# Mask transfers of one or two steps, and the queue of one block's inverse denominators, in a two-layer graph attention kernel

## The chip, the cores and the metric

The kernel runs on one core of a Trainium2 chip. The metric is the time in microseconds of one execution on the device, and the median over the runs is compared. A core has five engines with queues of their own: TensorE (PE in the profile, its weight loads PEld), VectorE (DVE), ScalarE (ACT), GpSimd (POOL) and SyncE (SP, which computes nothing and issues transfers). PE, DVE and ACT compute here; POOL mostly issues transfers, some of which add into their destination.

## The reference

There are 4096 nodes with 512 features in 4 heads of 128, and one adjacency matrix for both layers. Layer 0 is an encoder and a decoder with the same attention weights, layer 1 an ordinary graph attention:

```python
h = jnp.maximum(_layernorm(x), 0.0)
Xw = einsum('hnd,hde->hne', Xh, W)                   # Xh: h by heads
sig = sigmoid(f1[:, :, None] + f2[:, None, :])       # f1, f2: scores of a node, by head
att = masked_softmax(sig, adj != 0)                  # both patterns are adj
Xa = einsum('hij,hjd->hid', att, Xw)                 # encoder attention
emb = _mlp_block(_batchnorm(Xa), enc_mlp_W, ...)     # elu, residual, batch norm
Y = einsum('hij,hjd->hid', att, emb by heads)        # decoder attention, the same att
out = _mlp_block(elu(Y @ W^T), dec_mlp_W, ...)
x = x + out
# layer 1
h = jnp.maximum(_layernorm(x), 0.0)
feats = einsum('nf,hfo->hno', h, W1)
logits = leaky_relu(e_s[:, :, None] + e_n[:, None, :], 0.2) - 1e10 * (1 - A)
x = x + relu(softmax(logits) @ feats + b)
```

## The kernel before

All three attentions are one function, `attention`, called as "enc", "dec" and "gat". It works in eight **blocks**, one for each head `h` and half `tb` of the target nodes (`TB` = 2048), and a block in 32 **steps** `j` of 128 source nodes. A step makes one tile `e` of 128 x 2048 weights: in the encoder and the decoder ACT computes a tanh (line 579) and an exponential (580), and DVE multiplies by the mask (581); in the last attention ACT does one operation (1073) and DVE one with the mask in it (1074). Then PE multiplies `e` with the step's values (474 and 477 in the encoder and the last attention, 336 in the decoder).

**The masks.** Before the encoder begins, POOL's queue copies the adjacency from 32-bit floats to bytes in DRAM (`copy_adjacency`, eight casting transfers). SP loads the masks back: `mask_tile` takes one of three buffers, each of which holds the masks of two steps, and `load_mask` (line 217) fills it with one transfer of 512 KB. In every fifth step (`KEEP` = 5) the encoder stores its weights in DRAM, and the decoder reads these back instead of computing them; such a step needs no mask in the decoder, but its pair's transfer brings both. Three tiles for the encoder's first steps are loaded early, as `masks0`.

**The denominators.** The column sums of `e` are made in three ways, which lists of steps choose: POOL issues transfers that add halves of `e` into a sum (line 497, the "moved" steps), DVE adds `e` (505 and 507), or PE multiplies by ones (272). A block's sums are ready when it ends, and `ending` spreads the rest over the steps of the next block with `at(j, ...)`: `denominators` copies the sums from PSUM and stores them (`dens`), `columns` loads them as a column (`dcol`), `invert_them` inverts them on DVE (288 and 289), `inverses` stores the inverses (`rinvs`, line 292), and four `spread` load them, repeated for all partitions, into `rb` tiles (297). Then `scaled` (698) and `statistics` (701) work on the block's outputs on DVE. In the encoder and the decoder these small transfers are issued by POOL (`hop`), in the last attention by ACT. For the encoder's first block, whose ending runs in its second block, `slack` = 4 sets the steps back, and `dens` and `dcol` go on SP's queue; `rinvs` and `rb` go on POOL's.

The order within each engine's queue is laid out by the framework's scheduler from the order of the code, the dependencies, its own estimates of time and the explicit `issue_after` edges; an engine takes its queue in that order. `a_load` is the latest mask load, and the next row's load and a few extras are placed after it.

Of the kernel before, what the change touches and what calls it, by code (L numbers as in the profile page):

```python
# [45 lines left out]
TB = 2048  # L46
# [3 lines left out]
MG = 8  # L50
# [26 lines left out]
INVERT = 4  # L77
# [13 lines left out]
def kernel(ctx, tc, x, xT, adjT, w0, w0T, v0, wencT, wdecT, vecs, w1, w1T, a1, outT):  # L91
    nc = tc.nc
# [76 lines left out]
    masks = [[dram.tile([P, MG * TB], U8, name=f"mask{t}_{g}") for g in range(NJ // MG)] for t in range(NTB)]  # L169
# [41 lines left out]
    def mask_tile(keep):  # L211
        return keep.tile([P, 2 * TB], U8, name="a", bufs=3)

    def load_mask(a, tb, j):

        k = j % MG // 2
        return nc.sync.dma_start(a, masks[tb][j // MG][:, k * 2 * TB:(k + 1) * 2 * TB])

    @contextmanager
    def pinned(behind):  # L220
# [7 lines left out]
    def attention(what, keep, pools, weights, values, row_of, out, finish, ebufs, modes=None, invert=None,  # L228
                  kept=None, sums=None, sums2=None, extras={}, row0=None, masks0=(), in_parts0=1,
# [24 lines left out]
        spool, made, masks0 = pools, 0, list(masks0)  # L254
# [12 lines left out]
        hop = nc.scalar if kept is None else nc.gpsimd  # L267
# [20 lines left out]
            nc.vector.tensor_scalar(dcols[0], dcols[0], invert[0], None, invert[1])  # L288
            nc.vector.reciprocal(dcols[0], dcols[0])

        def inverses(h, tb, dcols):
            hop.dma_start(rinvs[h][tb].rearrange("o (p k) -> (o p) k", k=TB // P), dcols[0])

        def spread(h, tb, s):

            rb = spool.tile([P, IB], FP, name="rb", bufs=3 if fast is None else 2)
            hop.dma_start(rb, everywhere(rinvs[h][tb], 0, s * IB, IB))  # L297
            return rb

        def at(j, f, *args):  # L300

            later.setdefault(j, []).append(lambda: f(*args))

        def ending(h, tb, po, den, slack):

            outs = [out(spool, h, tb, s, po[s]) for s in range(SB)]
            if den is not None:

                dcols = []
                at(INVERT, denominators, h, tb, den, nc.sync if slack else hop)  # L310
                at(INVERT + (0 if hop is nc.gpsimd else 3) + slack // 2, columns, h, tb, dcols, nc.sync if slack else hop)
                at(INVERT + slack + (6 if hop is nc.gpsimd else 7), invert_them, dcols)
                at(INVERT + slack + (6 if hop is nc.gpsimd else 10), inverses, h, tb, dcols)
            rbs = {}
            for s, o in enumerate(outs):

                j = INVERT + slack + (7 if hop is nc.gpsimd else 11) + s % 2 + s // 2 * (7 if hop is nc.gpsimd else 5)
                at(j, lambda s=s: rbs.update({s: spread(h, tb, s)}))
                for k, f in enumerate(finish):
                    at(j + (6 + k if hop is nc.gpsimd else 3 + 3 * k),  # L320
                       lambda f=f, s=s, o=o: f(spool, h, tb, s, o, rbs[s], False))
# [78 lines left out]
        for n, (h, tb) in enumerate(blocks):  # L400
# [13 lines left out]
            adds, held, stores, at_end, next_row, two_masks = [], [], [], [], None, (None, None)  # L414
            for j in range(NJ):
# [11 lines left out]
                if store and kept == "read":  # L427
                    a_load = nc.sync.dma_start(e, ekeep[h][tb][j // KEEP])
                else:
                    if two_masks[0] != j // 2:  # L430
                        if masks0:
                            two, a_load = masks0.pop(0)
                        else:
                            two = mask_tile(keep)
                            a_load = load_mask(two, tb, j)
                        two_masks = j // 2, two
                    a = two_masks[1][:, j % 2 * TB:(j % 2 + 1) * TB]

                    with pinned([*(products_of[:1] if kept == "read" and n == 0 and j < 8 else ()),
                                 *(behind if n == 0 and j < EP else ())]):  # L440
                        products_of = weights(e, rowb, a, j, h, SB if NJ * n + j < in_parts0 else 1)


                    if stores and (store if n > 1 else j % KEEP == KEEP - 3):
                        k, t = stores.pop()
                        (nc.sync if n > 1 else nc.scalar).dma_start(ekeep[h][tb][k], t)
                    if store:
                        stores.append((j // KEEP, e))
# [137 lines left out]
    with tc.tile_pool(name="keep", bufs=1) as keep:  # L586

        with tc.tile_pool(name="f_small", bufs=1) as small, tc.tile_pool(name="f_work", bufs=2) as work:
# [29 lines left out]
            for ib in range(NIB):  # L618
                st = work.tile([P, C, 6], FP, name="st")
                mv = work.tile([P, C, 2], FP, name="mv")  # L620
                rstd = work.tile([P, C], FP, name="rstd")

                def deviations(lo, hi):

                    with pinned([first_hn] if ib == 1 or lo == 1 else []):
                        for c in range(lo, hi):
                            nc.vector.bn_stats(st[:, c, :], xs[ib][:, c, :])
                    for c in range(lo, hi):
                        nc.vector.bn_aggr(mv[:, c, :], st[:, c, :])
                    return rsqrt(rstd[:, lo:hi], mv[:, lo:hi, 1], LN_EPS)  # L630

                last_dve = deviations(0, 1 if ib == 0 else C)
                hT = work.tile([P, C, IB], FP, name="hT")
                for c in range(C):
                    if ib == 0 and c == 1:
                        last_dve = deviations(1, C)
                    by_pool = c == C - 1
                    hn = work.tile([P, F], FP, name="hn", tag="hnp" if by_pool else "hn")
                    made = (nc.gpsimd if by_pool else nc.vector).tensor_scalar(
                        hn, xs[ib][:, c, :], mv[:, c, 0:1], rstd[:, c:c + 1], ALU.subtract, ALU.mult)  # L640
                    if ib == 0 and not by_pool:
                        first_hn = made

                    if by_pool and ib > 0:
                        with tc.issue_after(made.ins):
                            copy_adjacency(ib - 1, half_loaded)
                            if ib == NIB - 1:
                                copy_adjacency(ib, half_loaded)
                    pt = bank().rearrange("p (f n) -> p f n", n=P)
                    for fb in range(C):  # L650
                        last_pe = nc.tensor.transpose(pt[:, fb, :], hn[:, fb * P:(fb + 1) * P], ident)
                    nc.scalar.activation(hT[:, :, c * P:(c + 1) * P], pt, AF.Relu)
                if ib == 0:

                    pw = bank1()
                    with tc.issue_after(last_pe.ins):
                        for h in range(H):
                            nc.tensor.matmul(pw[:, 2 * h:2 * h + 2], w0Ts[:, h, :], v0s[:, h, :],
                                             start=True, stop=True)
                    pwh = pw[:, 0:2 * H].rearrange("p (h s) -> p h s", s=2)  # L660
                    with tc.issue_after(last_dve.ins):
                        nc.vector.tensor_copy(w0x[:, :, D], pwh[:, :, 0])
                        nc.vector.tensor_scalar_mul(w0x[:, :, D + 1], pwh[:, :, 1], 0.5)
                for c in range(C):
                    j = ib * C + c
                    for k in range(2):
                        pv = heads_of(bank())
                        for h in range(2):
                            nc.tensor.matmul(pv[:, h, :], hT[:, 2 * k + h, c * P:(c + 1) * P], w0x[:, 2 * k + h, :],
                                             start=True, stop=True)  # L670

                        by_dve = ib + k >= NIB - 1
                        copied = (nc.vector.tensor_copy if by_dve else nc.scalar.copy)(
                            RS[:, 2 * k:2 * k + 2, j * D:(j + 1) * D], pv[:, :, 0:D])
                        if not by_dve:
                            last_copy = copied
                        nc.vector.tensor_copy(scores_of(j, k), pv[:, :, D:DX])
                if ib == SB - 1:
                    store_rows(rows[0], targets(0))
                    row0 = keep.tile([P, TB], FP, name="rowb", bufs=2)  # L680
                    row0_load = load_row(row0, rows[0], 0)
                    with tc.issue_after(row0_load.ins):
                        masks0 = []
                        for j in range(0, 6, 2):
                            a = mask_tile(keep)
                            masks0.append((a, load_mask(a, 0, j)))
            store_rows(rows[1], targets(1))


# [467 lines left out]
```

## Time and profile before

| what | value |
|---|---|
| median of 3 runs | 3191.95 us (3190.81 to 3193.84) |
| profiled execution | 3189.99 us, its span 3188.2 us |
| encoder attention, from its first product | 64.7 to 1034.9 us |
| decoder attention | 1174.7 to 2016 us |
| last attention | 2268 us to the end |
| mask loads | 384 of 512 KB, 4.9 us to land (median) |
| accumulating transfers of the encoder's sums | 142 of 512 KB, 7.6 us to land (median) |
| granted TensorE clock | 0.999 |

Lines of a timeline give the start and the duration in microseconds, the engine and line, the operation, its output and inputs, the number of merged instructions, and in square brackets the idle time of that engine just before, with what ended it. "DMA rb<-rinvs" as a releaser means that a transfer from `rinvs` into `rb` landed. The lines of a wait summary give a total in microseconds, the number of times, and the longest.

### The profile page before, as it was taken

How to read it: one execution, taken by the hardware profiler on the slowest of the kernel's cores; microseconds unless marked ns; L12 is line 12 of the kernel's file. 1: busy time of each engine (PE TensorE's matmuls, PEld its weight loads, DVE VectorE, ACT ScalarE, POOL GpSimd, SP SyncE). 2: the span in 40 equal slices, each digit the busy share in tenths (PEclk: the TensorE clock that was granted, in tenths of full speed). 3: DMA queues.
4: the chain of work that ended last, by engine and by line, in shares of the span. 5: the costliest groups of instructions: out<-in, count | busy, mean ns of one | idle time of the engine just before them, and what ended most of it. 6: DMA issues, size and time to landing. Idle time of an engine off the chain costs nothing.

```text
span 3188.2 us, 29265 instructions
## 1 busy us (share of the span) xinstructions
PE 3137.4 (98%) x10555; PEld 1369.9 (43%) x10555; DVE 2933.7 (92%) x2227; ACT 2574.2 (81%) x1830; POOL 520.1 (16%) x678
## 2 busy tenths in 40 slices
PE   7999999999999999999999999999999999999999
PEld 6444444434444463333333333458544444444444
DVE  7999999999999778999999999785699999999998
ACT  7999999999999449999999999466755656665663
POOL 3001211211211000010100100026312222122211
PEclk9999999999999999999999999999999999999999
DMA  9999978988988015545555555331579999899986
GB/s 214 204 199 248 270 200 231 260 224 229 264 225 214 24 47 165 168 156 187 172 176 172 171 183 162 92 112 64 155 187 233 217 222 240 219 212 236 229 209 173
DMA packets 167330, 603.07 MB, mean 189 GB/s; under 512 B 20672, under 2 KB 24016, under 8 KB 151184
## 3 DMA queue, kind: packets, MB, share of 16 engines
q0 software_dynamic: 70912, 231.92, 37.6%
q1 hardware_dynamic: 84112, 345.11, 31.5%
q10 hardware_dynamic: 12160, 24.16, 2.2%
q8 instruction: 83, 1.36, 0.2%
q14 instruction: 63, 0.52, 0.0%
HBM read 392.05 MB, written 84.30 MB: 149 GB/s over the span
## 4 chain that ended last, share of the span: by engine, by line
PE 69%; issue 11%; DVE 9%; DMA 6%; ACT 4%; POOL 0%; DVEq 0%; SPq 0%; ACTq 0%; POOLq 0%
PE ps L477 29%; PE ps L336 22%; PE ps L734 7%; PE den L336 3%; PE ps L979 3%; DVE e L581 3%; DMA w<-e 3%; DVE acc L507 3%; ACT e L579 2%; DMA acc<-e 2%; PE den L272 1%; ACT e L580 1%; DVE e L1074 1%; DVE R L507 1%; PE ps L817 1%
## 5 line engine op out<-in xcount | busy, mean ns | idle before, releaser
L477 PE MATMUL ps<-e,R 128*128 128x512 f32 x3992 | 1734.8, 594 | 24.4 <-DVE e L581 20.1
L477 PEld LDWEIGHTS ps<-e,R 128*128 128x128 f32 x3992 | 753.5, 190 | 1001.8 <-issue 926.0
L581 DVE TENSOR_TENSOR e<-e,a 128x2048 f32<-128x2048 f32 (+1 forms) x470 | 1048.1, 2259 | 70.5 <-ACT e L580 68.1
L579 ACT ACTIVATE e<-rowb,score 128x2048 f32<-128x2048 f32 (+1 forms) x470 | 909.6, 1970 | 21.8 <-PE ps L336 7.6
L580 ACT ACTIVATE e<-e 128x2048 f32<-128x2048 f32 (+1 forms) x470 | 866.8, 1880 | 3.4
L336 PE MATMUL ps<-e,R 128*64 128x512 f32 x2624 | 746.8, 592 | 1.6 <-DVE e L581 1.5
L1073 ACT ACTIVATE e<-rowb,nq,jcol 128x2048 f32<-128x2048 f32 x224 | 458.6, 2088 | 274.6 <-DMA w<-e 154.8
L1074 DVE SCALAR_TENSOR_TENSOR e<-e,jcol,a 128x2048 f32<-128x2048 f32 (+1 forms) x265 | 591.6, 2264 | 2.9 <-ACT e L1073 2.0
L336 PEld LDWEIGHTS ps<-e,R 128*64 128x64 f32 x2624 | 242.1, 137 | 319.6 <-issue 316.0
L507 DVE TENSOR_TENSOR R<-R,e 128x2048 f32<-128x2048 f32 x124 | 282.5, 2278 | 0.0
L507 DVE TENSOR_TENSOR acc<-acc,e 128x2048 f32<-128x2048 f32 x122 | 278.6, 2284 | 1.0
L497 POOL DMA_DIRECT2D w<-e x178 | 147.5, 834 | 613.8 <-DMA w<-e 390.4
L497 POOL DMA_DIRECT2D acc<-e x142 | 118.0, 873 | 701.2 <-DMA acc<-e 213.6
L734 PE MATMUL ps<-R,w 128*128 128x512 f32 x512 | 220.8, 593 | 0.6 <-DVE w L708 0.6
L734 PEld LDWEIGHTS ps<-R,w 128*128 128x128 f32 x512 | 97.1, 190 | 123.0 <-issue 116.9
L336 PE MATMUL den<-e,R 128*64 128x512 f32 x320 | 149.8, 592 | 0.0
L336 PE MATMUL ps<-e,w 128*64 128x512 f32 x288 | 138.1, 592 | 0.7 <-DVE e L581 0.7
L297 POOL DMA_DIRECT2D rb<-rinvs x60 | 34.8, 584 | 521.3 <-DVE R L698 450.2
L979 PE MATMUL ps<-w1x,hT 128*128 128x260 f32 x512 | 115.5, 384 | 0.7 <-ACT hT L957 0.7
L336 PE MATMUL ps<-t,w 128*64 128x512 f32 x336 | 111.3, 593 | 1.1 <-DVE t L345 1.1
L979 PEld LDWEIGHTS ps<-w1x,hT 128*128 128x128 f32 x512 | 96.6, 190 | 18.8 <-issue 3.3
L336 PE MATMUL ps<-t,R 128*64 128x512 f32 x192 | 90.2, 592 | 0.0
(207 smaller groups left out, 2111.1 us busy)
## 6 DMA issues: line engine op xcount, KB each, us to landing
a<-mask SPq DMA_DIRECT2D x384, 512.0 KB, 4.9
w<-e POOLq DMA_DIRECT2D x178, 512.0 KB, 7.1
acc<-e POOLq DMA_DIRECT2D x142, 512.0 KB, 7.6
e<-ekeep SPq DMA_DIRECT2D x48, 1024.0 KB, 7.1
ekeep<-e SPq DMA_DIRECT2D x36, 1024.0 KB, 7.6
mask<-in_adjT POOLq DMA_DIRECT2D x8, 2048.0 KB, 106.8
rowb<-rows SPq DMA_DIRECT2D x16, 1024.0 KB, 9.0
rb<-rinvs POOLq DMA_DIRECT2D x60, 256.0 KB, 4.8
```

The source lines that it names most:

```text
L297: hop.dma_start(rb, everywhere(rinvs[h][tb], 0, s * IB, IB))
L336: last_half = nc.tensor.matmul(b[g * HD:(g + 1) * HD, :], weight, x, start=start, stop=stop)
L477: last_main = nc.tensor.matmul(b, block(values[h], j), e[:, s * IB:(s + 1) * IB], start=(j == 0), stop=(j == NJ - 1))
L497: nc.gpsimd.dma_start(into_half, e_half, **({"accum_op": ALU.add} if j > moved[0] else {}))
L507: nc.vector.tensor_add(acc, acc, e)
L579: nc.scalar.activation(e, rowb, AF.Tanh, bias=column(score[:, 1], j, h), scale=0.5)
L580: last_act = nc.scalar.activation(e, e, AF.Exp, scale=0.5)
L581: last_dve = nc.vector.tensor_mul(e, e, a)
L734: last = nc.tensor.matmul(z, w[:, fb, o * P:(o + 1) * P], nodes(src[fb], ib), start=(fb == 0), stop=(fb == C - 1))
L979: m = nc.tensor.matmul(banks[k][:, 0:2 * DX], hT[:, fb, c * P:(c + 1) * P], w1x[:, fb, 2 * k:2 * k + 2, :].rearrange("p h x -> p (h x)"), ...
L1073: last_act = nc.scalar.activation(e, rowb, AF.Relu, bias=column(nq, j, h), scale=column(jcol, j, h))
L1074: last_dve = nc.vector.scalar_tensor_tensor(e, e, column(jcol2, j, h), a, ALU.add, ALU.mult)
```

## The change

A transfer of two steps' masks remains only in the encoder's first two blocks. Everywhere else each step that needs a mask loads its own half of the tile, with 2 KB instead of 4 KB in a row. In the encoder's first block's ending, the store of the inverses and the four loads that spread them are issued by SP instead of POOL, and these, with the operations that follow them, are set one step later.

```diff
-    def load_mask(a, tb, j):
-        k = j % MG // 2
-        return nc.sync.dma_start(a, masks[tb][j // MG][:, k * 2 * TB:(k + 1) * 2 * TB])
+    def load_mask(two, tb, j, n):
+        lo = j % 2 * TB
+        k = j % MG * TB
+        return nc.sync.dma_start(two[:, lo:lo + n * TB], masks[tb][j // MG][:, k:k + n * TB])
...
-                at(INVERT + slack + (6 if hop is nc.gpsimd else 10), inverses, h, tb, dcols)
+                at(INVERT + slack + (7 if slack else 6 if hop is nc.gpsimd else 10), inverses, h, tb, dcols,
+                   nc.sync if slack else hop)
...
-                j = INVERT + slack + (7 if hop is nc.gpsimd else 11) + s % 2 + s // 2 * (7 if hop is nc.gpsimd else 5)
-                at(j, lambda s=s: rbs.update({s: spread(h, tb, s)}))
+                j = INVERT + slack + (8 if slack else 7 if hop is nc.gpsimd else 11)
+                j += s % 2 + s // 2 * (7 if hop is nc.gpsimd else 5)
+                at(j, lambda s=s: rbs.update({s: spread(h, tb, s, nc.sync if slack else hop)}))
...
+                    at_once = 2 if kept == "write" and n < 2 else 1
                     if two_masks[0] != j // 2:
-                        if masks0:
-                            two, a_load = masks0.pop(0)
-                        else:
-                            two = mask_tile(keep)
-                            a_load = load_mask(two, tb, j)
+                        two, a_load = masks0.pop(0) if masks0 else (mask_tile(keep), None)
                         two_masks = j // 2, two
+                        if a_load is None:
+                            a_load = load_mask(two, tb, j, at_once)
+                    elif at_once == 1:
+                        a_load = load_mask(two_masks[1], tb, j, 1)
```

## The prediction

> **What bounds the kernel now.** I read the page's busy times first, then a table of busy time by stretch (one row per block of the first attention, one for the last), then the idle times of ScalarE in the first attention, and last the timelines of VectorE, GpSimd (POOL) and TensorE in its second block.
>
> ```profile
> PE 3137.4 (98%) x10555; PEld 1369.9 (43%) x10555; DVE 2933.7 (92%) x2227; ACT 2574.2 (81%) x1830; POOL 520.1 (16%) x678
> ```
>
> ```profile
> 194.09:319.50 125.41, 122.26 (x340) 50.84 (x336) 115.64 (x64) 123.61 (x68) 14.73 (x20) 0.99 0.96 230
> 436.40:556.90 120.50, 116.84 (x309) 49.44 (x305) 113.06 (x64) 116.10 (x64) 22.23 (x30) 1.00 0.87 235
> 676.80:795.80 119.00, 116.54 (x309) 49.50 (x305) 114.40 (x64) 119.00 (x65) 22.20 (x30) 1.00 0.88 238
> 1488.00:1593.00 105.00, 105.00 (x492) 35.14 (x490) 100.89 (x74) 102.19 (x61) 12.28 (x13) 1.00 0.53 173
> 2622.00:2735.00 113.00, 113.00 (x282) 48.95 (x281) 112.87 (x56) 69.82 (x42) 24.79 (x30) 1.00 0.93 220
> ```
>
> The columns of a stretch are its length, then busy time of PE, PEld, DVE, ACT and POOL, the clock, the DMA share and GB/s. PE is busy 3137.4 of 3188.2 us, so no edit can win more than 50.8 us, and 14.0 of those lie before the first attention's start at 64.67 (the table's rows from there to the end hold 3086.7 of PE's busy time) and 6.9 in its first block, where this edit changes nothing. In the decoder (105.00 of 105.00) and in the last attention (113.00 of 113.00) PE has no idle time, so a cheaper transfer there wins nothing; it can only lose. In encoder blocks 4 to 7 (counted from 1) PE idles 2.5 to 3.7 us a block, and there **ACT is the bound**: 119.00 of 119.00 in the third row shown. Time is won in the encoder only by taking waits from ACT. ACT's waits from 300 to 1040 us (total, times, longest):
>
> ```profile
> ACT e L579 <- DMA acc<-e: 6.9, 6, 2.4
> ACT e L579 <- PE den L272: 1.2, 1, 1.2
> ```
>
> Six times ACT waited for a weight tile that an accumulating transfer still read: 2.41, 1.52 and 0.47 us in block 4, 0.99 and 0.68 in block 5, 0.80 in block 7. The other wait is at the end of block 2, which holds one more of 0.38 us for an accumulation, at 273. Now block 2, where the first block's inverse denominators travel:
>
> ```profile
> 240.37 0.24 DVE L289 RECIPROCAL dcol<-dcol 128x16 f32<-128x16 f32 x1
> 266.41 0.69 DVE L698 TENSOR_TENSOR R<-R,rb 128x512 f32<-128x512 f32 x1 [4.44 <-DMA rb<-rinvs]
> ...
> 234.28 1.11 POOL L497 DMA_DIRECT2D acc<-e  x2 [181.45 <-issue]
> 253.07 0.89 POOL L292 DMA_DIRECT2D rinvs<-dcol  x1
> 259.85 1.65 POOL L297 DMA_DIRECT2D rb<-rinvs  x3 [5.89 <-DMA rinvs<-dcol]
> 261.46 1.85 POOL L497 DMA_DIRECT2D acc<-e  x2
> ...
> 277.16 24.71 PE L477 MATMUL ps<-e,R 128*128 128x512 f32 x56 [1.11 <-DVE e L581]
> 303.77 12.26 PE L477 MATMUL ps<-e,R 128*128 128x512 f32 x24 [1.90 <-DVE e L581]
> 317.10 2.01 ACT L579 ACTIVATE e<-rowb,score 128x2048 f32<-128x2048 f32 x1 [1.25 <-PE den L272]
> ```
>
> The inverses are ready at 240.6, but POOL, idle in the trace until 234 behind the adjacency casts, issues them at 253.07, holds everything until they land, and spreads them at 259.85. DVE stands 4.44 us. After that it runs without a gap to 329, PE loses 1.11 and 1.90 us to it, and so PE's column sums come late and ACT stands 1.25 us.
>
> **What the Trainium skill says.** All four places are in "DMA: Bandwidth & Descriptors". (1) "Issuing engines are not separate DMA queues": transfers of all engines run on the same 16 DMA engines; another issuer saves issue time alone. The trace agrees on issue time (rinvs 0.87 us on POOL, 0.33 on ACT's queue) but shows more, since POOL's issue was 12.5 us late by what stood ahead of it. (2) "Anatomy of one DMA": a DMA's wait for a semaphore happens on the issuing sequencer. The 5.89 us above, with the accumulations behind, are that. (3) "Queues, rings and completion order": an engine goes round its rings, packet by packet. The trace fits: a 4 KB packet of the hardware queue takes 156 ns at least and 202 on the mean. (4) "Why small descriptors are slow": a fixed few cycles per packet. Here 2 KB takes 81 ns at least, so two cost 162 against 156.
>
> **The inverses, part by part.** One store (8 KB) and four loads (256 KB) leave POOL's queue for SP's, each one step later. Issue falls from 0.87 + 4 x 0.55 = 3.1 us of POOL to 5 x 0.33 = 1.6 us of SP. The store can go at 240.7. Its landing: SP's one small store of this kind, dens at 198.35, let the next issue at 206.23, 7.9 us; with 4.8 (median on ACT's queue) as the near bound and POOL's worst wait of 10.0 as the far one, the spreads issue at 245.5 to 251 and land some 5.8 us later (median of rb), by 257. DVE wants them at 262, or about 3.7 us later by the step that is added. **The 4.44 us go**; what is late next is ACT, which runs gapless there. PE's 1.11 + 1.90 = 3.0 us go with them, but ACT gains only its own waits, 1.25 + 0.38 = 1.6 us, and from 303 to 908 the encoder follows ACT. PE's earlier sums also start block 4's accumulations earlier, by up to 3.0 - 1.6 = 1.4 us. So 1.6 to 3.0; I take 2.0.
>
> The new wait is on SP: behind a store that hasn't landed stand mask loads. A load is issued when its tile's former pair is done and needed two pairs, 4 x 3.7 = 14.8 us, later; it lands in 4.9. That leaves 9.9 us, against a delay of at most 10 less the time until the next load is due (243.4, 2.8 us after the inverses). No stall, then; without that cover, up to 3 us. The last spread also waits for DVE's first scaling to free an rb tile (three, shared with dsb); loads behind it have the same 9.9 us. The next row's 1 MB load (243.83) is needed at 315. POOL gets its 5.89 us wait back, so block 2's accumulations run some 8 us earlier: this is what takes ACT's 0.38.
>
> **The masks, part by part.** Loads: before 3 x 128 = 384. After: 2 x 16 in the first two blocks, 6 x 32 in the other encoder blocks, 8 x 26 in the decoder (six steps of 32 read kept weights), 8 x 32 in the last attention: 688. 304 more issues of 0.32 us are 97 us of SP, which is no compute engine's. Decoder bytes fall by 8 x 6 x 0.26 = 12.6 MB; that stage has a DMA share of 0.53 and a full PE, so nothing is won. DVE waits for a mask in every step instead of every second: the semaphore instructions of such a wait (21 to 50 ns) lie under the running multiply in the trace (starts stay 2.26 us apart), so nothing is lost.
>
> What isn't shown is how 2 KB packets change the accumulations (7.6 us median to land; POOL's queue waits for each). Where a mask meets one, each of its 8 packets per DMA engine stands behind 81 instead of 156 ns: 0.6 us at most for one accumulation. The two halves can use their tile at the same moment, so the second half may hit the next accumulation, and then nothing is won. Four or five in a row lie before block 4's waits. The bounds: all 6.9 us of ACT's waits go, or none and some are added (below). I take 2.8, since four of the six waits are under 1 us. In the last attention's start DVE waited 0.80 us for the first mask, which comes sooner by half: 0.2 kept, as ACT is the next wait there (1.04).
>
> **Sum.** 2.0 + 2.8 + 0.2 = 5.0 us. The profiled execution took 3189.99 (span 3188.2 and 1.8 around it), 1.96 less than the median of the runs, 3191.95; its expected successor is 3185.0, and from the median 3187.0.
>
> **Rivals.** (a) All of ACT's waits go: 1.6 + 6.9 + 0.8 = 9.3 us, **3182.7**. For it: block 6 already runs with none, so they are marginal. Against: POOL still waits 7.7 to 10 us in each later block for dens and rinvs. (b) The halves leave as one burst, packets don't matter, only the inverses count: 2.0 us, **3190**. For it: the tile's release frees both halves. (c) Slower: the DMA engines become the bound. A pair costs an engine 16 x 81 + 9 instead of 8 x 156 ns, 57 ns more, 0.9 us a block. DMA share is 0.93 in the last attention; an accumulation by halves takes 8 x 0.31 x 2 = 5 us of each 6.9 us there, and ACT is only 0 to 1.3 us ahead of DVE in the first steps of a block, DVE about one step ahead of PE. If each of 14 blocks pays: +12.8 - 1.6 = 11 us, **3203**. It decides from the point where the lag of the accumulations isn't made up in the steps that have none (28 to the next block's 3, some 17 us); that slack speaks against it, as does ACT's lead of 5 to 16 us in mid block. (d) The queue orders shift and POOL's gain is lost to SP's wait: **3192**.
>
> **How the numbers follow.** 0.2% is 6.4 us, about what a measurement of this kernel can tell from no change. Main case 0.42, at 3187; (a) 0.25; (b) 0.13; (c) 0.10; (d) 0.10. Beyond 3185.6 lie (a) and a third of the main case: faster 0.38. Slower is (c) and a little of (d), 0.12; within, 0.50. The range runs from under (a), 3181, over (d) to 3196; (c) is left out.
>
> **What would show it.** Right: no DVE wait for rb near 262, rinvs on SP at about 241, PE's idle in 194 to 320 near 0 instead of 3, ACT's total on accumulations under 4, 688 mask issues, PE full in decoder and last attention. Wrong: a DVE wait for a mask in block 2; ACT waits on accumulations at 6.9 or more; PE idle after 2509, or the accumulations' median landing over 7.6.

## The result, and the profile after

The changed kernel took **3182.14 us** (median of 8 runs, 3180.5 to 3186.22), the kernel before 3191.73 beside it: a ratio of **0.9973, 95% interval 0.9962 to 0.9984**. That is 0.27% faster, with an interval of 0.16 to 0.38%: more than the 0.2% of the forecast by the middle value, though not by the whole interval. The forecast had held a gain under 0.2% for likelier (0.50) than one over it (0.38). The time is 4.9 us below the predicted one, inside the range, and within 0.6 us of rival (a), "all of ACT's waits go". The profiled execution took 3180.92 us, its span 3179.1. Line numbers above 217 are higher by 1 to 4 than before (477 is now 481, 579 is 583, 581 is 585).

Engines of the page, then the five stretches that were shown of before, each moved to the same block (columns as there):

```profile
PE 3138.7 (99%) x10555; PEld 1371.4 (43%) x10555; DVE 2932.4 (92%) x2227; ACT 2574.0 (81%) x1830; POOL 520.8 (16%) x673
```

```profile
194.40:315.70 121.30, 120.01 (x340) 50.42 (x336) 115.00 (x64) 120.94 (x66) 11.39 (x14) 1.00 0.97 234
433.60:551.60 118.00, 116.59 (x312) 49.50 (x304) 114.39 (x65) 118.00 (x65) 22.23 (x30) 1.00 0.89 241
669.70:787.90 118.20, 116.58 (x308) 49.49 (x304) 114.36 (x64) 118.20 (x65) 22.20 (x29) 1.00 0.89 241
1480.00:1585.00 105.00, 105.00 (x492) 35.17 (x490) 100.86 (x74) 102.93 (x62) 13.24 (x13) 1.00 0.49 158
2614.00:2727.00 113.00, 113.00 (x281) 49.05 (x280) 113.00 (x56) 70.82 (x41) 24.96 (x31) 1.00 0.94 224
```

No engine has noticeably less to do. Block 2 is 4.1 us shorter (121.30 against 125.41) and block 4 2.5 (118.00 against 120.50). ACT is busy for all of blocks 4 and 6. In ScalarE's waits between 60 and 1040 us, those for accumulations (6.9 us after 300 us before, and 0.4 in block 2) are down to one of 0.2 us, and that on the end of block 2 is gone:

```profile
ACT e L583 <- DMA acc<-e: 0.2, 1, 0.2
```

The timelines of block 2: VectorE, SyncE (SPq), then TensorE.

```profile
241.17 0.25 DVE L290 RECIPROCAL dcol<-dcol 128x16 f32<-128x16 f32 x1
...
267.09 0.69 DVE L702 TENSOR_TENSOR R<-R,rb 128x512 f32<-128x512 f32 x1
...
270.95 2.29 DVE L585 TENSOR_TENSOR e<-e,a 128x2048 f32<-128x2048 f32 x1 [0.97 <-DMA a<-mask]
```

```profile
241.45 0.32 SPq L293 DMA_DIRECT2D rinvs<-dcol  x1
248.53 0.88 SPq L298 DMA_DIRECT2D rb<-rinvs  x2
249.52 0.36 SPq L218 DMA_DIRECT2D a<-mask  x1
250.40 0.32 SPq L209 DMA_DIRECT2D rowb<-rows  x1
250.78 1.38 SPq L298 DMA_DIRECT2D rb<-rinvs  x1
253.13 12.19 SPq L218 DMA_DIRECT2D a<-mask  x3
```

```profile
261.69 42.65 PE L481 MATMUL ps<-e,R 128*128 128x512 f32 x99
305.63 7.13 PE L481 MATMUL ps<-e,R 128*128 128x512 f32 x16 [1.29 <-DVE e L585]
```

DVE's first scaling (267.09) no longer waits. The new loss is at 270.95: the mask load of 253.13, queued behind the spreads, a row of 1 MB and an earlier mask, landed 17.8 us after its issue, and PE paid 1.29 us for it later.

**Where the 9.1 us of the two spans are.** The marks are the starts of TensorE's last sum product of a block (`den<-acc`, line 272, now 273), and of its first and last product with layer 1's weights. Block 1 takes 0.8 us more, blocks 2 to 7 take 9.0 less (720.7 to 711.7), block 8 is equal, from there to the end of layer 1's projection 0.6 more, and from there to the end 1.5 less (925.4 to 923.9).

**What the clock adds to it.** The fourteen profiles told of here have up to five stretches each, most of them 3.4 us long, in which TensorE was granted half its clock (those at the very end left out). Block 8 shows the price: it takes 120.1 us in every profile without such a stretch in it, 121.8 in the five with one, and 123.5 in the third experiment's, whose stretch is of 6.8 us. The profile before has one stretch and the one after two, so they don't make the gain. But that of before lies at 304.7 us, near the end of block 2: four multiplications take 839 to 854 ns there instead of 429, 1.7 us in all, and ACT's wait of 1.25 us for PE's column sums follows at 317.1. The prediction put that wait down to PE's idle time behind the late inverses alone; but the clock's 1.7 us are more than the whole wait. In the second experiment, in which DVE still waits 1.8 us for the inverses and PE 2.3 us for DVE, there is no stretch at half clock in block 2 and ACT has no such wait. The stretch begins about 1 us after PE's idle of 1.90 us, and three others of the encoder (experiments 5, 8 and 11) begin as soon after one of 1.9; so the late inverses may have set it off. But six more idles of 1.9 us in the encoder of these profiles have none after them, so the 1.25 us aren't a sure part of what the inverses cost.

The last part is a wait that the prediction hadn't seen. TensorE's timeline at the start of the last attention's third block, before and after:

```profile
2507.34 1.98 PE L474 MATMUL ps<-e,R 128*128 128x512 f32 x4 [1.18 <-ACT R L1079]
```

```profile
2498.39 1.88 PE L478 MATMUL ps<-e,R 128*128 128x512 f32 x4
```

PE needed a bank of PSUM that ACT emptied late, since ACT had waited for accumulations (`w<-e`, 3.04 us just before). This wait of PE shows in seven of the eight profiles with pairs in the last attention that are told of here (0.3 to 1.5 us) and in none of the six with one-step loads; from the projection's end to the kernel's, the eight take 925.0 us on the mean, the six 923.9.

### The profile page after: what moved, and what is told of

The parts are those of the page before. It is cut to its first block, busy times and chain, and to the rows that moved or that the text cites. A ratio compares the mean times of both kernels' runs of the same rounds, so it can differ in the third digit from the quotient of the medians.

```text
span 3179.1 us, 29792 instructions
## 1 busy us (share of the span) xinstructions
PE 3138.7 (99%) x10555; PEld 1371.4 (43%) x10555; DVE 2932.4 (92%) x2227; ACT 2574.0 (81%) x1830; POOL 520.8 (16%) x673
## 3 DMA queue, kind: packets, MB, share of 16 engines
q1 hardware_dynamic: 128608, 333.60, 30.5%
## 4 chain that ended last, share of the span: by engine, by line
PE 76%; DVE 12%; issue 5%; ACT 4%; DMA 1%; DVEq 0%; SPq 0%; ACTq 0%; POOL 0%; POOLq 0%
PE ps L481 40%; PE ps L339 18%; PE ps L738 7%; DVE e L585 5%; PE ps L983 3%; DVE acc L511 3%; PE den L339 3%; PE den L273 2%; ACT e L583 2%; ACT e L584 1%; DVE R L511 1%; PE ps L821 1%; DVE e L1078 1%; PE ps L478 1%; PE ps L673 1%
```

## The experiments

Three theories stand against each other. **Packets**, the prediction's: 2 KB records let accumulations through sooner (a record is one entry of the trace's DMA packets, here one row of a transfer). **Position**: a second half stands later in SyncE's queue, behind the 1 MB store of kept weights. **Count**: it takes two transfers. Each run's ratio is against the kernel before on the same chip; it is not the quotient of the two medians, from which it differs by up to 0.0005. "ACT's waits" are those of the profile before 900 us, and the last column is the time of blocks 2 to 7 by PE's sum products.

| kernel | median us (before there) | ratio, interval | ACT's waits | blocks 2 to 7 |
|---|---|---|---|---|
| before | 3191.73 | 1 | 8.5 | 720.7 |
| the change | 3182.14 (3191.73) | 0.9973, 0.9962 to 0.9984 | 0.2 | 711.7 |
| 1 inverses only | 3186.22 (3190.11) | 0.9988, 0.9980 to 0.9996 | 5.4 | 717.3 |
| 2 masks only | 3183.67 (3190.11) | 0.9980, 0.9972 to 0.9987 | 0.2 | 711.7 |
| 3 one transfer, 2 KB records | 3187.08 (3190.11) | 0.9990, 0.9982 to 0.9998 | 5.1 | 716.7 |
| 4 one step in the encoder only | 3182.68 (3190.11) | 0.9978, 0.9969 to 0.9987 | 1.4 | 712.9 |
| 5 halves by partitions | 3188.80 (3191.65) | 0.9992, 0.9984 to 1.0000 | 6.8 | 718.9 |
| 6 both halves together | 3183.50 (3191.65) | 0.9974, 0.9966 to 0.9982 | 1.6 | 712.5 |
| 7 all inverses on SyncE, pairs | 3184.25 (3191.65) | 0.9975, 0.9965 to 0.9986 | 2.9 | 714.7 |
| 8 one step everywhere | 3192.46 (3191.65) | 1.0001, 0.9993 to 1.0009 | 8.7 | 715.4 |
| 9 inverses, stores halved | 3186.49 (3189.08) | 0.9990, 0.9983 to 0.9997 | 1.8 | 713.3 |
| 10 the change, stores halved | 3180.93 (3189.08) | 0.9973, 0.9963 to 0.9984 | 1.0 | 712.6 |
| 11 pairs in the first block only | 3181.63 (3189.08) | 0.9972, 0.9961 to 0.9984 | 2.3 | 713.9 |
| 12 as 3 | 3184.42 (3189.08) | 0.9987, 0.9980 to 0.9994 | 2.2 | 713.0 |

**The last two columns carry the accounting**: but for the eighth, the length of these blocks less ACT's waits lies between 710.8 and 712.2 us in every profile. By itself this says little, since any engine with a fixed amount of work leaves the same remainder when its idle time is taken off. What makes ACT the bound is that nothing else is left to take off: after the change it stands 0.2 of 711.7 us. What the encoder loses there is ACT's waits.

**1 and 2, each part alone.** The first is the kernel before with the diff's `inverses` and `spread` alone, the second the change with these two left as before.

> The kernel before with the inverses' part alone: store and spreads of the first block's inverses on SP, one step later; all masks as before, two steps in one transfer. Theory A (as the prediction had it: the inverses win 2 to 3 us, the smaller mask transfers take ScalarE's waits for accumulations in blocks 4 to 7): about 3189, and ScalarE still waits 5 to 7 us on accumulations from 300 to 1040 us. Theory B (the inverses do it all, because the earlier second block shifts the accumulations of the later blocks): about 3183.5, ScalarE's waits near 0, and only the 1.1 us of the last attention's start missing.

> The masks' part alone: one step in a transfer except in the first two encoder blocks; the inverses stay on GpSimd's queue. Theory A: ScalarE's waits on accumulations after 300 us fall from 6.9 to under 1.5 us, the 4.44 us of VectorE and the 1.25 us of ScalarE in block 2 remain; about 3185. Theory B: the waits stay near 6.9 us and only the start of the last attention gains 1.1 us; about 3190.5.

ScalarE's waits, first kernel, then second:

```profile
ACT e L581 <- DMA acc<-e: 3.8, 4, 1.9
ACT e L581 <- DVE e L583: 1.6, 1, 1.6
```

```profile
ACT e L581 <- DMA acc<-e: 0.2, 1, 0.2
```

By the medians the inverses bring 3.9 us and the masks 6.4, together 10.3 against the 9.6 of both: nearly a sum. By the intervals the inverses bring 1.3 to 6.4 us and the masks 4.1 to 8.9. The masks alone take nearly all of ACT's waits, in blocks that the inverses don't touch.

**3 and 12, one transfer with 2 KB records.** The first experiment's kernel, in which a tile has a gap of 16 bytes between its halves, so that a pair's transfer falls into 2 KB pieces:

```diff
+        return nc.sync.dma_start(a.rearrange("p (m i) -> p m i", m=2)[:, :, 0:TB],
+                                 src.rearrange("p (m i) -> p m i", m=2))
```

> The inverses' part, and masks in one transfer for two steps everywhere, but outside the first two encoder blocks with a gap of 16 bytes between the steps in the tile, so that the packets have 2 KB as in the change; number and moment of the transfers are as before. If the packet size is what frees the accumulations, ScalarE's waits are as small as after the change (under 1 us) and the time is the change's plus the 1.1 us of the last attention's start, about 3183. If two transfers are needed, it runs like the inverses alone (about 3189 under theory A).

> The third experiment's kernel once more, beside others of the same chip: inverses on SyncE, a pair's masks in one transfer with a gap between its halves, so 2 KB packets. If the packets' size alone had helped and the third experiment was a scatter: 3182 to 3184 and ScalarE's waits for accumulations under 2 us. If the number of transfers is what counts: 3186 to 3187 and waits of 3 to 6 us, as before.

```profile
ACT e L588 <- DMA acc<-e: 5.1, 7, 1.3
```

```profile
ACT e L588 <- DMA acc<-e: 2.2, 3, 0.8
```

Twice the ratio is that of the inverses alone (0.9990 and 0.9987 against 0.9988): **the records' size brings nothing by itself that these runs can tell**; each interval is about 2.5 us wide to either side. The twelfth met neither of its forecasts (3184.42 us, waits of 2.2), and its runs fall apart, eleven at 3182.1 to 3184.5 us and six at 3186.3 to 3189.8; why is open. The two profiles are of the same kernel and show how far its waits scatter; the second was its fastest run but one. A verdict on waits from one profile would have gone wrong here.

**4, one-step loads in the encoder only.**

```diff
-                    at_once = 2 if kept == "write" and n < 2 else 1
+                    at_once = 1 if kept == "write" and n >= 2 else 2
...
-                            a_load = load_mask(two, tb, j, at_once)
+                            a_load = load_mask(two, tb, j - j % 2 if at_once == 2 else j, at_once)
```

> The change, but with one-step mask transfers in encoder blocks 3 to 8 alone; decoder and last attention load two steps in one transfer as before. The decoder's 12.6 MB are expected to be worth nothing (TensorE is full there) and the last attention's start 1.1 us: 1.1 us above the change, about 3183.2, with ScalarE's waits in the encoder as small as after the change.

3182.68 us, a ratio 0.0005 above the change's, inside both intervals. PE's wait on ACT in the last attention is back (0.6 us), and the last part takes 924.8 us. The decoder's smaller traffic wins no time: from the encoder's end to layer 1's projection it is 1102.4 us here and 1102.9 in the change. It even has a cost that no forecast named. In the decoder DVE waits for kept weights to land (`e<-ekeep`), 9.4 to 10.4 us in the eight profiles with pairs there and 12.0 to 17.5 in the six with one-step loads. PE lost nothing to it in the change, but 2.8 us in the sixth experiment's profile and 1.6 in the eighth's.

**5, two transfers of 64 partitions.** The first experiment's kernel with

```diff
+                            a_load = load_mask(two, tb, j - j % 2, 2, slice(0, P if at_once == 2 else P // 2))
+                            if at_once == 1:
+                                load_mask(two, tb, j - j % 2, 2, slice(P // 2, P))
```

> The inverses on SyncE, and every pair of masks that the change would load by halves is loaded in two transfers of 64 partitions each, issued one right after the other at the place of the pair's one transfer; rows stay 4 KB. If it is the number of transfers (each transfer's packets leave room for others) that quickened the accumulations: about 3182, ScalarE's waits for accumulations under 1 us, as in the changed kernel. If it is where the second half stands in SyncE's queue, behind the store of kept weights: as the first experiment, 3186, waits of 3 to 6 us, and GpSimd's waits for the small store of the inverses at 6 to 9 us in the blocks that store weights.

In the decoder a pair stays one transfer here.

```profile
ACT e L583 <- DMA acc<-e: 6.8, 7, 1.7
```

ACT waited 6.8 us and nothing was won. But it is no clean test of the count. The queues in 436 to 905 us of the first kernel, then of this one (packets, MB, share of the 16 engines' time):

```profile
q1 hardware_dynamic: 13104, 62.92, 37.1%
```

```profile
q1 hardware_dynamic: 14096, 62.92, 41.0%
```

The same bytes took a tenth longer: a 4 KB mask record 223 ns on the mean instead of 194. The Trainium skill ("DMA: Bandwidth & Descriptors", "Rules for kernel authors") calls two transfers to disjoint halves of the partitions not worth the bother, since they share the same engines; here the records even took longer.

**6, both halves together.** The change, with both halves issued at the even step:

```diff
-                    elif at_once == 1:
-                        a_load = load_mask(two_masks[1], tb, j, 1)
+                            if at_once == 1 and j % 2 == 0 and not (kept == "read" and j % KEEP == KEEP - 2):
+                                load_mask(two, tb, j + 1, 1)
```

> The change, but both halves of a pair are loaded one right after the other at the even step, so that no other transfer of SyncE's queue (a store of kept weights, the next row) comes between them. If the second half's later place in SyncE's queue is what helps: about 3186 to 3187, ScalarE's waits for accumulations 3 to 6 us, GpSimd's waits for the inverses' store in blocks 4 to 7 at 6 to 9 us. If two separate transfers suffice wherever they stand: about 3182, waits under 1 us, and GpSimd's waits near 4.5 us.

```profile
ACT e L583 <- DMA acc<-e: 1.6, 2, 1.1
```

All the gain of the change without the position: 0.9974. **Position falls.** Against the third experiment the bytes, the size of the records, the places in SyncE's queue and the moment of issue (the halves of all 64 pairs in blocks 4 to 7 go under 1 us apart) are the same in the encoder; the number of transfers, and with it the order of the records, is not. The intervals of the third and the twelfth (from 0.9982 and 0.9980) and of this one (to 0.9982) overlap by 0.0002 at most. The comparison isn't of the encoder alone: about 1 us of this kernel's gain (0.0003) is the last attention's, and against it stand the 2.8 us of its profile's decoder.

**7, all inverses on SyncE.** Pairs as before, but `hop` is SyncE for the inverses and spreads of every encoder block:

```diff
-                   nc.sync if slack else hop)
+                   nc.sync if slack or kept == "write" else hop)
...
```

The `-` line is that of the first experiment's kernel; `spread` is changed in the same way.

> Pair masks as before, and the inverses' store and the four spreads of every encoder block on SyncE's queue, so that GpSimd's queue never waits for an inverse store to land. If it is this wait of GpSimd, with the accumulations queued behind it, that makes ScalarE wait: ScalarE's waits for accumulations go to under 1 us with 4 KB pairs, time 3182 or less unless the masks behind SyncE's wait come late (VectorE would then wait for masks, over 2 us in a block, and the time be 3186 or more). If the masks' own transfers delay the accumulations: waits stay at 3 us or more, 3186.

This was to test another reading: that POOL's wait for the small store of the inverses, with accumulations behind it, makes ACT wait. That wait in block 4, before and after the change:

```profile
460.19 0.87 POOL L292 DMA_DIRECT2D rinvs<-dcol  x1
470.80 1.11 POOL L297 DMA_DIRECT2D rb<-rinvs  x2 [9.73 <-DMA rinvs<-dcol]
```

```profile
459.15 0.58 POOL L293 DMA_DIRECT2D rinvs<-dcol  x1 [2.06 <-DVE dcol L290]
463.90 1.61 POOL L298 DMA_DIRECT2D rb<-rinvs  x3 [4.17 <-DMA rinvs<-dcol]
```

In blocks 4 to 7 POOL waits 9.7, 8.0, 5.5 and 7.3 us for it before, 4.2, 4.2, 4.5 and 5.5 after, 4.1, 4.1, 4.7 and 5.6 in the sixth experiment, 5.3 to 8.8 in the third. Summed over the four blocks it is 18.4 to 23.2 us in the seven profiles with one-step loads there, 24.6 to 30.5 in the five with pairs in one transfer, and 22.0 in the fifth experiment. Without the wait, and with 512 KB pairs, the ratio is 0.9975 (0.9965 to 0.9986), and of ACT's waits this is left, 1.3 us of it in block 2 and 1.6 in block 5:

```profile
ACT e L581 <- DMA acc<-e: 2.9, 2, 1.6
```

The forecast of this theory, under 1 us, wasn't met, and the ratio's interval overlaps that of the inverses alone (0.9980 to 0.9996). So **that POOL's queue stands behind its small store is a likely part of ACT's waits**, and getting it out of the way may win about as much as the change; it isn't shown to be the whole. The other profiles speak against a simple rule: POOL waited 4.9 to 6.0 us for the store in the fifth, with 6.8 us of ACT's waits, and 5.8 to 7.9 in the twelfth, with 2.2.

**8 and 11, where the pairs are needed.** One-step loads everywhere, then everywhere but in the first block (`n < 1` for `n < 2`).

> The change, with one-step mask loads in the encoder's first two blocks too, but for the three tiles loaded early. If the pairs there only save issues: 3182, as the change. If SyncE's wait for the inverses in block 2 makes single halves late: VectorE waits for masks there grow from 1.0 to several us, and the time is 3183 to 3186. If less is in the rings ahead of a half: VectorE's wait of 0.97 us in block 2 goes and the time is 3181.

> The change, with two steps' masks in one transfer in the encoder's first block only. The casts of the adjacency run until about 234 us, into the second block. If halves lose wherever the casts' packets share the rings: block 2 takes about 4 to 6 us longer than the changed kernel's 121.3 us, its masks land in 10 us or more until 234, time 3186 to 3188. If the loss with halves everywhere came from the first block alone: 3182 to 3183.

Mask loads issued in 64 to 195 us and their median landing, the change, then the eighth kernel, and the eighth kernel's VectorE waits for masks from 60 to 330 us (1.0 us in the change):

```profile
a<-mask SPq DMA_DIRECT2D x17, 512.0 KB, 9.8
```

```profile
a<-mask SPq DMA_DIRECT2D x32, 256.0 KB, 15.5
```

```profile
DVE e L585 <- DMA a<-mask: 15.5, 12, 3.3
```

Beside the casts half the bytes take longer. The trace's packet records don't name the DMA engine, but a record of another queue often starts 3 or 4 ns before a mask record ends, which can be taken as the next one on its engine. Where exactly one record started there, it was another queue's in all 1905 cases of 4 KB masks and all 3367 of 2 KB masks: the queues take turns record by record, and half a record in each turn is half the bytes. All gain is lost, which no expectation foresaw: of the 10.2 us between the two profiles 7.8 are lost by the encoder's end and 2.5 more in the decoder and the projection. In the eleventh kernel, block 2 takes 125.2 us, 3.9 more, about what I had reckoned for the casts (though a half-clock stretch at 307.9 us, worth up to 1.7, is in it), yet the time is the change's. ACT lost 1.5 us there; the rest of what DVE and PE lost was made up in blocks 3 and 4 (116.9 and 116.4 us, against 117.9 and 118.0): the encoder followed ACT, not PE. The first block alone needs pairs.

**9 and 10, the stores of kept weights in two transfers,** in the first experiment's kernel and in the change:

```diff
+                            nc.sync.dma_start(ekeep[h][tb][k][:, :TB // 2], t[:, :TB // 2])
+                            nc.sync.dma_start(ekeep[h][tb][k][:, TB // 2:], t[:, TB // 2:])
```

> The first experiment's kernel (inverses on SyncE, masks in pairs of 512 KB) with each store of kept weights that SyncE issues in blocks 3 to 8 (1 MB, 8 KB in a row) made in two transfers of 1024 columns each. If any transfer of SyncE's queue lets the accumulations through sooner when it is cut in two full-width transfers: ScalarE's waits for accumulations under 2 us instead of 3.8, time 3183 to 3184. If it is particular to the masks: waits 4 to 6 us, 3186. If smaller packets of the stores take more turns from the accumulations: waits over 6 us, 3189.

> The change, with the stores of kept weights of blocks 3 to 8 in two transfers as well: could be the fastest version. ScalarE has 0.24 us of waits for accumulations left in the changed kernel's profile, so by the theory that ScalarE's waits are all there is to win, 3182 and no gain; if the stores still cost something that the waits don't show, 3180; if more transfers crowd the rings, 3184 or more.

Neither gains on its parent (0.9990 against 0.9988, 0.9973 against 0.9973). The ninth's profile has only 1.8 us of ACT's waits and blocks 2 to 7 of 713.3 us, yet that run took 3187.82 us, with five half-clock stretches, all outside these blocks; its median says no as well. So two transfers for one isn't a rule for every transfer of the queue, and no version here beats the change: with ACT's waits at 0.2 us, the encoder has none left to give.

## Why the prediction was right, and where not

**The bound: right.** ACT bounds the encoder, and taking its waits is what paid. Of the 9.0 us that blocks 2 to 7 lost, 8.3 are ACT's waits; 1.25 of these follow the half-clock stretch and aren't surely the change's.

**The inverses: right in mechanism, the size not settled.** Taken at 2.0 with an end at 3.0, they measured 3.9 alone, but the interval, 1.3 to 6.4 us, holds 2.0 as well. The 4.44 us of DVE went, the store went out at 241.45 (240.7 was reckoned), the spreads at 248.53 (245.5 to 251), and PE's idle in the block fell to 1.3. The 1.25 us at the block's end went, but the half-clock stretch has a share in it (above); the 0.38 became 0.24, but 0.70 with the inverses alone, so that "this is what takes ACT's 0.38" failed. If a term was too small, it is "PE's earlier sums also start block 4's accumulations earlier": with the inverses alone, block 4's waits fell from 4.40 to 1.86 us. That is one profile each, of waits that scatter by 3 us within one kernel, and so not shown.

**"No stall, then": wrong, by 0.97 us of DVE and 1.29 of PE.** The prediction had named "a DVE wait for a mask in block 2" as a sign of being wrong. SyncE stood behind the store until 248.53, as allowed for; but "it lands in 4.9" was a median of the whole kernel, and with the row and the spreads just ahead the load took 17.8. ACT didn't wait for it, so it cost the sum nothing.

**The masks: the step that failed.** 2.8 us stood for what measured 6.4 alone (4.1 to 8.9). The step reckoned what a record costs an accumulation, "81 instead of 156 ns", "0.6 us at most for one", and took the 6.9 us of waits as six separate ones to be shortened. Experiments 3 and 12 speak against the records' size as the cause, and one meeting isn't all that can stretch these waits: POOL's queue goes on only when its small store has landed, and its waits of 5.5 to 9.7 us fell to 4.2 to 5.5. I had noted these waits, against rival (a), as 7.7 to 10 us for both small stores; for the inverses block 6's was 5.5. Rival (a) priced the outcome well, 9.3 us against 9.6 by the medians, but for it spoke only that block 6 ran without waits, and its 1.25 us at the end of block 2 hung on a stretch of the clock, so the nearness is in part luck.

**The Trainium skill's place (3).** "Queues, rings and completion order" says that an engine drains a whole packet, some 9 to 17 descriptors, before it turns to another ring. I read the records of the trace as these packets. Beside the casts all 1905 and all 3367 mask records whose next one could be told were followed by another queue's. In blocks 4 to 7, told in the same way, a mask record with an accumulation's record ahead of it was followed by another queue's in 132 of 152 cases of the first experiment, 109 of 126 of the third and 396 of 424 of the sixth. The measurement decides: turns are of one record here. Then, by the prediction's working, the third kernel should have won as the sixth did, and it didn't. **Why two transfers help where one with the same records doesn't stays open.** What can be said is that more mask records followed one of an accumulation (424 such cases in the sixth and 313 in the change, against 126 and 228 in the third and the twelfth, the same kernel twice).

**The last attention: right in sign, wrong in place.** I gave 0.2 us to the first mask; after seven multiplications DVE stands where it stood before (8.9 us after `jcol` was made). The 1 us lies at the third block's start, which "PE has no idle time" had read over: the window shown began later.

**Costs of nothing: right in this profile, with less margin in the decoder.** The decoder is full as before (105.00 of 105.00), 656 and 32 mask loads were issued, and no loss to SyncE's 304 more issues shows. But DVE's longer waits for kept weights there reached PE in two of the six profiles with one-step loads (experiments 6 and 8), so "a cheaper transfer there wins nothing; it can only lose" was, for the decoder, nearer the truth than a cost of nothing:

```profile
a<-mask SPq DMA_DIRECT2D x656, 256.0 KB, 4.6
acc<-e POOLq DMA_DIRECT2D x142, 512.0 KB, 7.2
a<-mask SPq DMA_DIRECT2D x32, 512.0 KB, 10.0
```

**Rival (c), DMA engines as the bound, fell.** In the last attention the accumulations landed in 6.7 us instead of 7.1, and PE waits less.

## What to carry to other kernels

Where one engine runs without gaps but for its waits, add these up and expect their stretch of the kernel to follow them; then ask for each what stands ahead of its releaser in the queue that issues it, small stores too. A transfer beside a competing queue is to be judged by what it meets: here smaller mask rows lost beside the casts and two transfers won beside the accumulations. Waits of a single profile scatter (5.1 and 2.2 us for one kernel), so a cause of a few us needs medians beside it. And before a small wait is put down to the work ahead of it, look at the granted clock there: a stretch of 3.4 us at half clock stood before the 1.25 us here, and a kernel without it had no such wait.

## What the hardware showed that I had not expected

Beside the casts the DMA queues took turns record by record (1905 of 1905 and 3367 of 3367 cases that could be told), which gives smaller records a smaller share: 512 KB in 4 KB records landed in 9.8 us, 256 KB in 2 KB records in 15.5. And a load of half the partitions took 223 ns for a 4 KB record, against 194 for one of all. TensorE's half-clock stretches cost 1.7 us each where PE is full: block 8 took 120.1 us without one, 121.8 with one.
